# The last attention and the int8 feed forward of a decoder, from two loops one after the other to one loop with a turn per sequence

## The chip, the cores and the metric

The kernel runs on one core of a Trainium2 chip. A core has five engines with a queue each: TensorE (PE) multiplies matrices and writes to the banks of PSUM; VectorE (DVE), ScalarE (ACT) and GpSimd (POOL) work element by element, the first two also on PSUM; SyncE (SP) issues transfers (DMA). An engine works through its queue in order, and where an instruction needs another engine's result it waits on a semaphore, with all that is behind it. The metric is the time of one execution on the device, in microseconds (us); the time before is the median of three runs.

## The reference, cut to what matters

The model is a decoder of four layers, each an attention, a second attention over a context and a feed forward, twelve stages in all. Behind every stage comes `x = layernorm(x + stage(x))`. There are 16 sequences of 128 tokens with 256 features, in float32. The change touches the last two stages:

```python
def L3_xattn(q, k, v, gamma):             # q = x, k = v = context; (16, 128, 256)
    # eight heads over the middle axis: 16 tokens to a head; the softmax runs over the 256 features
    qh = q.reshape(B, 8, 16, 256); kh = k.reshape(B, 8, 16, 256); vh = v.reshape(B, 8, 16, 256)
    sm = softmax(einsum('bhdq,bhdl->bhql', qh, kh) / sqrt(16), axis=-1)
    return gamma * einsum('bhql,bhdl->bhdq', sm, vh).reshape(B, 128, 256)

def L3_ffn(x, W1, B1, W2, B2):            # 256 -> 1024 -> 256
    X1_q, sX1 = quantize_rowwise(x)       # round(x * 127 / absmax of the token)
    W1_q, sW1 = quantize_global(W1)       # one absmax for the whole matrix
    X2 = gelu((X1_q @ W1_q.T) * (sX1 * sW1 / 127**2) + B1)
    X2_q, sX2 = quantize_rowwise(X2)
    W2_q, sW2 = quantize_global(W2)
    return (X2_q @ W2_q.T) * (sX2 * sW2 / 127**2) + B2

x = layernorm(x + L3_xattn(x, ctx, ctx, gamma))
x = layernorm(x + L3_ffn(x, W1, B1, W2, B2))
```

Every sequence goes through these two stages by itself: nothing passes between sequences, except that the two weights are quantised once.

## The kernel before, in words

The whole activation `X` (128 tokens on the partitions, 16 sequences, 256 features) stays in on-chip memory. `run` opens the stages in order, each with pools of its own; the weights of a stage are loaded while the stage before it works. PSUM's eight banks are shared out by stage: in stage 10 the pool behind `ps` has six (bankA in the profile), the one behind `pt` two (bankB). A bank is given out in turn and can be written again when the reader of its last content is done.

**Stage 10, the attention** (`width_attention`, `width_unit`). One unit is one sequence `b`, written as a generator whose `yield`s cut it into pieces:

- the loads of three 256 KB context tiles by SP (L1857 to L1859);
- two pieces of score maxima: PE multiplies X with `eo` into four banks, DVE reduces each bank to a maximum in `npad`;
- PE transposes `npad`, DVE adds the maxima to the masked X (`xp`);
- two pieces of scores: eight matmuls into four banks, and four exponentials by ACT into `e`;
- two pieces of values: 16 matmuls of `vp` and `e` into one bankB, which ACT copies to `o`;
- PE transposes `o`, DVE takes reciprocals `rr` of the sums, POOL spreads them times gamma into `rw`;
- PE transposes `rw`, DVE multiplies (`y`), POOL adds both halves of `y` to X.

`rota` writes the order out by hand: in turn `n` it takes one piece of unit `n - lag` for each lag in a list. `Ordered` keeps each engine to that order; SP's transfers are left free. Behind every fourth unit `finish_in_turns` normalises four sequences: moments on DVE, the power -1/2 on POOL, the normalisation on DVE, and eight transposes with two ACT copies into `xT`. Buffers are three to five deep, `npad` and `rw` three each.

**Stage 11, the feed forward** (`s11`). First the weights: for each of the two matrices DVE finds the largest magnitude of each partition, POOL the largest over partitions, DVE scales and rounds (adding and subtracting `MAGIC`, L2306 and L2308). Then groups of four sequences: DVE quantises the tokens (`quantise`, L1953 to L1960: maximum, reciprocal, scaling, `t`, rounding `q`), PE transposes, ACT copies (`xqT`); then for each sequence PE multiplies with W1 into two banks, DVE scales and adds the bias (`h`, L2328), ACT applies gelu (L2332), DVE quantises the 1024 hidden values, PE transposes them in eight blocks, ACT copies (`hqT`, L2340), PE multiplies with W2, DVE scales and adds the bias (`y`, L2345), POOL adds to X (L2346). Behind each group come the normalisation and one 512 KB output transfer (L451). Nothing here is held to the written order.

A line of the profile can be a helper's: all ordered instructions have L321, so they are told apart by their tiles.

Of the kernel before, what the change touches and what calls it, by code (L numbers as in the profile page):

```python
# [12 lines left out]
F32 = mybir.dt.float32  # L13
BF16 = mybir.dt.bfloat16
# [6 lines left out]
NB = 16  # L21
S = 128
D = 256
# [300 lines left out]
class Decoder:  # L324
# [141 lines left out]
    def run(self):  # L466
# [4 lines left out]
        weights = {}  # L471
# [1362 lines left out]
    def s10(self, wk, w, last):  # L1834
        self.width_attention(wk, self.row("s10_gamma"), last)

    def width_attention(self, wk, gamma, last):
        nc = self.nc
        npad = [wk.tile([128, 512], F32, name=f"npad7_{n}", bufs=1) for n in range(3)]
        rw = [wk.tile([128, 2, 2, 128], F32, name=f"rw7_{n}", bufs=1) for n in range(3)]  # L1840
        for t in npad + rw:
            nc.gpsimd.memset(t, 0.0)
        self.nc = Ordered(self.tc, nc)
        rota(
            [self.width_unit(wk, gamma, npad[b % 3], rw[b % 3], b, last) for b in range(NB)],
            [0, 1, 3, 2, 4, 1, 3, 2, 4, 1, 5, 6, 7],
        )
        self.nc = nc

    def width_unit(self, wk, gamma, npad, rw, b, last):  # L1850
        nc = self.nc
        scale = 0.25
        eo = wk.tile([128, 2, D], F32, tag="eo7", name="eo7", bufs=3)
        e1 = wk.tile([128, 2, D], F32, tag="e17", name="e17", bufs=4)
        vp = wk.tile([128, 2, 8, 32], F32, tag="vp7", name="vp7", bufs=5)
# [4 lines left out]
        yield  # L1860
        xb = self.X[:, b, :]
# [17 lines left out]
        xp = wk.tile([128, 2, D], F32, tag="xp7", name="xp7", bufs=3)  # L1879
# [6 lines left out]
        e = wk.tile([128, 2, 4, 2, D], F32, tag="e7", name="e7", bufs=3)  # L1886
# [19 lines left out]
        o = wk.tile([128, 2, D], F32, tag="o7", name="o7", bufs=3)  # L1906
# [22 lines left out]
        if b % 4 == 3:  # L1929
            yield  # L1930
            yield from self.finish_in_turns(b // 4, last)
# [362 lines left out]
    def s11(self, wk, w, last):  # L2294
        nc = self.nc
        wq, sw = {}, {}
        for n in ("w1", "w2"):
            src = w[n].rearrange("p a b -> p (a b)")
            am = wk.tile([128, 1], F32, name=f"am_{n}", bufs=1)
            nc.vector.tensor_reduce(am, src, AX.X, ALU.max, apply_absolute_value=True)  # L2300
            al = wk.tile([128, 1], F32, name=f"al_{n}", bufs=1)
            nc.gpsimd.partition_all_reduce(al, am, 128, bass_isa.ReduceOp.max)
            s = wk.tile([128, 1], F32, name=f"s_{n}", bufs=1)
            nc.vector.reciprocal(s, al)
            nc.vector.tensor_scalar(s, s, 127.0, None, ALU.mult)
            nc.vector.tensor_scalar(src, src, s, MAGIC, ALU.mult, ALU.add)  # L2306
            q = wk.tile(list(w[n].shape), BF16, name=f"q_{n}", bufs=1)
            nc.vector.tensor_scalar(q, w[n], MAGIC, None, ALU.subtract)  # L2308
            nc.vector.tensor_scalar(al, al, 1.0 / (127.0 * 127.0), None, ALU.mult)
            wq[n], sw[n] = q, al  # L2310
        for g in range(NG):
            xq, am, _ = self.quantise(wk, self.X[:, 4 * g : 4 * g + 4, :], "11x")
            c1 = self.sm(4, tag="c111")
            nc.vector.tensor_scalar(c1, am, sw["w1"], None, ALU.mult)
            p = self.pt(2, 4, 128, dtype=BF16)
            for j in range(4):
                for k in range(2):
                    nc.tensor.transpose(p[:, k, j, :], xq[:, j, 128 * k : 128 * k + 128], self.identb)
            xqT = wk.tile([128, 2, 4, 128], BF16, tag="xqT11", name="xqT11")
            nc.scalar.copy(xqT, p)  # L2320
            for j in range(4):
                b = 4 * g + j
                h = wk.tile([128, 1, 1024], F32, tag="h11", name="h11")
                for n in range(2):
                    p = self.ps(512)
                    for k in range(2):
                        self.mm(p, xqT[:, k, j, :], wq["w1"][:, k, 512 * n : 512 * n + 512], k, 2)
                    nc.vector.scalar_tensor_tensor(  # L2328
                        h[:, 0, 512 * n : 512 * n + 512], p, c1[:, j : j + 1],
                        self.row("s11_b1")[:, 512 * n : 512 * n + 512], ALU.mult, ALU.add,  # L2330
                    )
                nc.scalar.activation(h, h, AF.Gelu_apprx_tanh)  # L2332
                hq, am2, _ = self.quantise(wk, h, "11h")
                c2 = self.sm(1, tag="c211")
                nc.vector.tensor_scalar(c2, am2, sw["w2"], None, ALU.mult)
                p = self.pt(8, 128, dtype=BF16)
                for k in range(8):
                    nc.tensor.transpose(p[:, k, :], hq[:, 0, 128 * k : 128 * k + 128], self.identb)
                hqT = wk.tile([128, 8, 128], BF16, tag="hqT11", name="hqT11")
                nc.scalar.copy(hqT, p)  # L2340
                p = self.pt(D)
                for k in range(8):
                    self.mm(p, hqT[:, k, :], wq["w2"][:, k, :], k, 8)
                y = wk.tile([128, D], F32, tag="y11", name="y11")
                nc.vector.scalar_tensor_tensor(y, p, c2, self.row("s11_b2"), ALU.mult, ALU.add)  # L2345
# [20 lines left out]
```

## Time and profile before

| what | value |
|---|---|
| median of 3 runs | 4087.18 us (4083.28 to 4091.48) |
| the profiled execution | 4093.2 us |
| its span in the profile | 4091.4 us |
| first matmul of stage 10 | at 3781.9 us |
| last addition to X in stage 10 | ends at 3951.0 us |
| first h of stage 11 | at 3965.7 us |
| last normalisation of stage 11 | ends at 4087.3 us |
| table loads on ACT from 3640 us to the end | 1 |

The profile is of one execution. Times of instructions count from the start of its span. The busy time of an engine is the time in which it works; its waits are put down to the instruction of another engine that came last. The two stages of the change are the last 310 us; everything ahead of them, 92% of the span, is the same code in both kernels. The clock granted to PE stands beside the windows, as a share of full speed.

### The profile page before, as it was taken

How to read it: one execution, taken by the hardware profiler on the slowest of the kernel's cores; microseconds unless marked ns; L12 is line 12 of the kernel's file. 1: busy time of each engine (PE TensorE's matmuls, PEld its weight loads, DVE VectorE, ACT ScalarE, POOL GpSimd, SP SyncE). 2: the span in 40 equal slices, each digit the busy share in tenths (PEclk: the TensorE clock that was granted, in tenths of full speed). 3: DMA queues.
4: the chain of work that ended last, by engine and by line, in shares of the span. 5: the costliest groups of instructions: out<-in, count | busy, mean ns of one | idle time of the engine just before them, and what ended most of it. 6: DMA issues, size and time to landing. Idle time of an engine off the chain costs nothing.

```text
span 4091.4 us, 96512 instructions
## 1 busy us (share of the span) xinstructions
PE 3615.8 (88%) x39274; PEld 2188.1 (53%) x39282; DVE 2572.0 (63%) x5650; ACT 2022.5 (49%) x4535; POOL 1846.0 (45%) x2036
## 2 busy tenths in 40 slices
PE   6999999999998716798989989888999999998975
PEld 4666666566565404565446655564454554554543
DVE  3767677677774464565235547665677666675776
ACT  2666666666665212343124544425565665564442
POOL 1444444444443135752135542204786666666221
PEclk8999999999999857899979999988999999999986
DMA  2111111111110001100010012101111111111200
GB/s 81 35 36 41 35 36 39 35 38 37 35 40 20 29 1 42 43 12 15 0 60 27 27 65 94 61 1 50 35 40 40 40 40 35 40 40 59 88 17 21
DMA packets 120649, 156.47 MB, mean 38 GB/s; under 512 B 15440, under 2 KB 79696, under 8 KB 119824
## 3 DMA queue, kind: packets, MB, share of 16 engines
q1 hardware_dynamic: 114352, 143.59, 11.4%
q8 instruction: 311, 5.10, 0.5%
q10 hardware_dynamic: 5712, 5.19, 0.4%
q0 software_dynamic: 144, 1.52, 0.1%
q14 instruction: 130, 1.06, 0.1%
HBM read 131.64 MB, written 2.10 MB: 33 GB/s over the span
## 4 chain that ended last, share of the span: by engine, by line
PE 76%; DVE 10%; ACT 5%; POOL 5%; issue 2%; DMA 1%; SPq 0%; ACTq 0%; POOLq 0%; DVEq 0%
PE bankA L321 39%; PE bankB L321 20%; PE bankC L321 8%; PE bankA L462 5%; PE bankB L462 4%; ACT accq L321 1%; DVE X L321 1%; ACT ot L321 1%; ACT gT L321 1%; POOL var L321 1%; DVE npad L321 1%; POOL t L321 1%; PE bankB L427 0%; POOL ln_rs L402 0%; ACT eb L321 0%
## 5 line engine op out<-in xcount | busy, mean ns | idle before, releaser
L321 PE MATMUL bankA<-xT,wzx 128*128 128x512 f32 x1024 | 458.5, 601 | 0.0
L321 DVE SCALAR_TENSOR_TENSOR acc<-bankA,half,acc 128x508 f32<-128x508 f32 (+2 forms) x384 | 285.2, 743 | 168.1 <-ACT acc L321 159.1
L321 POOL TENSOR_TENSOR m<-m,gm 128x512 f32<-128x512 f32 x256 | 318.1, 1278 | 45.3 <-ACT m L321 45.3
L321 PEld LDWEIGHTS bankA<-xT,wzx 128*128 128x128 f32 x1024 | 190.2, 191 | 227.2 <-issue 188.9
L321 PE MATMUL bankA<-xT,wkq 128*128 128x512 f32 x512 | 259.7, 632 | 0.0
L321 POOL TENSOR_TENSOR gT<-yx,sz 128x512 f32<-128x512 f32 x128 | 160.6, 1275 | 211.9 <-DVE yx L321 211.8
L321 PE MATMUL bankA<-xT,wvg 128*128 128x512 f32 x512 | 250.5, 612 | 0.2 <-issue 0.2
L321 POOL TENSOR_TENSOR eb<-eb,c_tri_s 128x512 f32<-128x512 f32 x64 | 81.3, 1271 | 375.3 <-ACT eb L321 375.3
L321 ACT ACTIVATE e<-bankA 128x512 f32<-128x512 f32 x320 | 165.2, 602 | 158.8 <-PE bankA L321 158.7
L321 DVE TENSOR_REDUCE npad<-bankA 128x2 f32<-128x512 f32 (+1 forms) x320 | 198.5, 684 | 60.9 <-PE bankA L321 60.6
L321 PE MATMUL bankC<-gT,wo 128*128 128x512 f32 x512 | 233.4, 599 | 2.7 <-POOL gT L321 2.7
L321 ACT ACTIVATE m<-bankA 128x512 f32<-128x512 f32 x256 | 132.1, 603 | 157.4 <-PE bankA L321 157.4
L321 POOL TENSOR_TENSOR sq<-sq,s 128x512 f32<-128x512 f32 x124 | 157.8, 1272 | 58.5 <-ACT s L321 53.8
L321 POOL TENSOR_SCALAR rs_ve<-o_mv 128x4 f32<-128x4 f32 x64 | 34.6, 540 | 291.7 <-DVE o_mv L321 291.7
L321 DVE SCALAR_TENSOR_TENSOR vT<-th,accv 128x512 f32<-128x512 f32 x64 | 45.6, 712 | 185.6 <-ACT th L321 185.6
L321 PEld LDWEIGHTS bankB<-y,tt 32*32 32x32 f32 x8192 | 87.0, 107 | 123.6 <-issue 88.5
L321 DVE SCALAR_TENSOR_TENSOR yx<-xs,cols,bankB 128x512 f32<-128x512 f32 x128 | 95.1, 747 | 91.9 <-PE bankB L321 86.3
L321 DVE SCALAR_TENSOR_TENSOR acck<-bankA,half_cols,acck 128x508 f32<-128x508 f32 (+2 forms) x192 | 142.5, 742 | 13.3 <-ACT acck L321 6.9
L321 PEld LDWEIGHTS bankC<-gT,wo 128*128 128x128 f32 x512 | 93.8, 192 | 99.3 <-issue 94.4
L321 DVE SCALAR_TENSOR_TENSOR accq<-bankA,half_cols,accq 128x508 f32<-128x508 f32 (+2 forms) x192 | 142.3, 741 | 4.5
L321 DVE SCALAR_TENSOR_TENSOR accv<-bankA,half_cols,accv 128x508 f32<-128x508 f32 (+2 forms) x192 | 140.0, 729 | 4.5
L321 ACT ACTIVATE acc<-bankA,half 128x512 f32<-128x512 f32 x128 | 100.7, 787 | 83.0 <-PE bankA L321 83.0
(482 smaller groups left out, 9321.9 us busy)
## 6 DMA issues: line engine op xcount, KB each, us to landing
wzx<-in_s_wzx SPq DMA_DIRECT2D x64, 512.0 KB
up<-cums SPq DMA_DIRECT2D x1152, 2.0 KB
wkq<-in_s_w SPq DMA_DIRECT2D x64, 256.0 KB
wvg<-in_s_w SPq DMA_DIRECT2D x64, 256.0 KB
wo<-in_s_wo SPq DMA_DIRECT2D x64, 128.0 KB
sw<-qraw SPq DMA_DIRECT2D x64, 128.0 KB
eo<-in_ctx_eo SPq DMA_DIRECT2D x32, 256.0 KB
e<-in_ctx_e SPq DMA_DIRECT2D x32, 256.0 KB
```

The source lines that it names most:

```text
L321: return lambda *a, **k: self.tc.keep_in_program_order(f(*a, **k))
L462: self.nc.tensor.matmul(out, lhsT=lhsT, rhs=rhs, start=(k == 0), stop=(k == n - 1))
```

## The change

Stage 10 (when it isn't the last) now runs both stages. A unit is a pair for one sequence: `width_unit` for the attention, `s11_unit` for the feed forward, and `weave` runs their pieces in an order of 21 places, `(which, lag)`, written out by hand. In turn `n` the place `(A, 1)` takes the next piece of the attention of sequence `n - 1`, and `(B, 9)` one of the feed forward of sequence `n - 9`. `s11` itself then does nothing.

```diff
     def s10(self, wk, w, last):
-        self.width_attention(wk, self.row("s10_gamma"), last)
...
+        npad, rw = self.width_zeros(wk, 1, 1)
+        _, w11 = self.weights[11]
+        with self.tc.tile_pool(name="kk11", bufs=2, side="right") as wk11:
+            self.nc = Ordered(self.tc, nc)
+            first = self.s11_weights(wk11, w11)
+            units = [
+                (
+                    self.width_unit(
+                        wk, self.row("s10_gamma"), npad[b % len(npad)], rw[b % len(rw)], b, None,
+                        [2, 3, 4, 2, 2, 1], first,
+                    ),
+                    self.s11_unit(wk11, w11, b),
+                )
+                for b in range(NB)
+            ]
+            A, B = 0, 1
+            weave(units, [
+                (A, 1), (A, 4), (A, 0), (B, 9), (A, 1), (B, 6), (A, 3), (B, 9), (A, 3), (B, 7), (B, 5),
+                (A, 2), (A, 1), (B, 4), (A, 3), (B, 6), (B, 7), (B, 5), (A, 1), (B, 5), (B, 4),
+            ])
```

Read by pieces, a turn holds in this order: A's first maxima (lag 1), the product and additions (4), the loads (0), B's last moments (9), A's second maxima (1), gelu (6), the first values (3), the last normalisation and output (9), the second values and the copy `o` (3), the transposes of the hidden values and `hqT` (7), the quantisation of the tokens (5), the second scores (2), the transposes of `npad` and `xp` (1), the first moments (4), the transposes of `o`, `rr` and `rw` (3), the quantisation of the hidden values (6), the second product, `y` and the addition (7), the transposes of the tokens and `xqT` (5), the first scores (1), the matmuls and `h` (5), the first normalisation (4).

The attention's unit keeps its work, with three differences. Its buffers are fewer (`npad` and `rw` one each, `eo` 2, `e1` 3, `vp` 4, `xp` 2, `e` 2, `o` 1). In the first maxima's piece it takes one step of the weights' preparation, as long as there is one. And it doesn't normalise: the `finish_in_turns` behind every fourth unit, with its transposes into `xT`, is gone.

```diff
         yield
+        if more:
+            next(more, None)
...
-        if b % 4 == 3:
+        if b % 4 == 3 and last is not None:
             yield
             yield from self.finish_in_turns(b // 4, last)
```

The feed forward goes by single sequences, and some of DVE's work goes to POOL: both roundings of the quantisation, the rounding of the weights, the two scalings `c1` and `c2`, and the normalisation.

```diff
+    def layernorm(self, b):
+        xb = self.X[:, b, :]
+        mv, rstd = self.moments([xb], 1e-5, "ln")
+        yield
+        self.nc.gpsimd.tensor_scalar(xb, xb, mv[:, 0, 0:1], rstd[:, 0:1], ALU.subtract, ALU.mult)
+
+    def quantise_row(self, wk, src, m, tag, bufs):
...
+        nc.vector.tensor_reduce(am, src, AX.X, ALU.max, apply_absolute_value=True)
+        nc.vector.reciprocal(s, am)
+        nc.vector.tensor_scalar(s, s, 127.0, None, ALU.mult)
+        t = wk.tile([128, m], F32, tag="t" + tag, name="t" + tag)
+        nc.vector.tensor_scalar(t, src, s, MAGIC, ALU.mult, ALU.add)
+        q = wk.tile([128, m], BF16, tag="q" + tag, name="q" + tag, bufs=bufs)
+        nc.gpsimd.tensor_scalar(q, t, MAGIC, None, ALU.subtract)
+        return q, am
+
+    def s11_unit(self, wk, w, b, norm=True):
...
+            yield from self.layernorm(b)
+            yield
+        xq, am = self.quantise_row(wk, xb, D, "11x", 1)
+        c1 = self.sm(1, tag="c111")
+        nc.gpsimd.tensor_scalar(c1, am, w["s1"], None, ALU.mult)
+        yield
...
+        xqT = wk.tile([128, 2, 128], BF16, tag="xqT11", name="xqT11", bufs=1)
+        nc.scalar.copy(xqT, p)
+        yield
...
+            nc.vector.scalar_tensor_tensor(h[:, cs], p, c1, self.row("s11_b1")[:, cs], ALU.mult, ALU.add)
+        yield
+        nc.scalar.activation(h, h, AF.Gelu_apprx_tanh)
+        yield
+        hq, am2 = self.quantise_row(wk, h, 1024, "11h", 1)
...
+        yield
...
+        hqT = wk.tile([128, 8, 128], BF16, tag="hqT11", name="hqT11", bufs=1)
+        nc.scalar.copy(hqT, p)
+        yield
...
+        nc.vector.scalar_tensor_tensor(y, p, c2, self.row("s11_b2"), ALU.mult, ALU.add)
+        nc.gpsimd.tensor_tensor(xb, xb, y, ALU.add)
+        yield
+        yield from self.layernorm(b)
+        nc.sync.dma_start(self.out[b], xb)
```

The weights' preparation (`s11_weights`) is a generator too, of four steps: for each matrix, first the maxima (DVE, POOL), then the scaling (DVE) and the rounding (now POOL). The output goes out in 16 transfers of 128 KB. The arithmetic of both stages is the same.

## The prediction

> **What bounds the kernel now.** I read the page first. Its shares (PE 88%, DVE 63%) are averages over twelve stages, and only the last two change, so next I cut the end of the span into windows. Columns: start:end, length, then busy us of PE, weight loads, DVE, ACT and POOL with counts, the granted clock, DMA share, GB/s.
>
> ```profile
> 3823.00:3850.00 27.00, 27.00 (x296) 14.80 (x288) 20.68 (x41) 14.15 (x27) 7.94 (x12) 1.00 0.30 90
> 3951.00:3967.00 16.00, 5.63 (x22) 3.31 (x24) 15.39 (x35) 3.47 (x4) 2.50 (x4) 0.50 0.00 1
> 3967.00:4087.00 120.00, 63.03 (x336) 38.22 (x336) 91.16 (x218) 35.78 (x35) 19.00 (x24) 0.63 0.04 14
> ```
>
> The first window is the attention in full flow: PE busy all of it at full clock, a sequence every 8.77 us in the timeline. The second prepares the feed forward's weights: DVE alone. The third is the feed forward: DVE busy 76%, PE only 53% at clock 0.63, 7.5 us a sequence. So the attention is bound by PE and the feed forward by DVE and its waits, one after the other. The attention's first matmul starts at 3781.9 and the span ends at 4091.4: the part that changes takes 309.5 us. Everything before 3781.9 is the same code.
>
> Next, the groups by shape in the last stages, and POOL's groups in the whole kernel (busy us, mean ns of one | idle before), for the price of each instruction:
>
> ```profile
> L321 DVE TENSOR_REDUCE npad<-bankA 128x2 f32<-128x512 f32 x128 | 79.4, 684 | 21.0 <-PE bankA L321 21.0
> L321 ACT ACTIVATE e<-bankA 128x512 f32<-128x512 f32 x128 | 66.1, 602 | 62.3 <-PE bankA L321 62.3
> L2328 DVE SCALAR_TENSOR_TENSOR h<-bankA,c,rows 128x512 f32<-128x512 f32 x32 | 22.4, 744 | 0.0
> L1953 DVE TENSOR_REDUCE am11h<-h 128x1 f32<-128x1024 f32 x16 | 19.1, 1212 | 0.1
> L1959 DVE TENSOR_SCALAR t11h<-h,s11h 128x1024 f32<-128x1024 f32 x16 | 11.9, 744 | 0.0
> L321 POOL TENSOR_SCALAR gT<-gT 128x512 f32<-128x512 f32 x64 | 96.1, 1501 | 23.7 <-ACT gT L321 18.9
> L321 POOL TENSOR_SCALAR xd<-xd,qsx 128x256 f32<-128x256 f32 x16 | 18.4, 1150 | 46.8 <-DVE xd L321 20.0 <-PE bankB L321 18.0 <-DVE xp L321 8.5
> L1569 POOL TENSOR_SCALAR d<-d5i 128x1280 f32<-128x1280 int32 x1 | 3.5, 3452 | 3.3 <-PE bankB L321 3.3
> L2346 POOL TENSOR_TENSOR X<-X,y 128x256 f32<-128x256 f32 x16 | 13.7, 856 | 103.1 <-DVE y L2345 86.8 <-DVE s11h L1954 13.1 <-DVE s11x L1954 3.1
> ```
>
> **The change, engine by engine.** A full turn holds one attention unit and one feed forward unit, in a fixed order on every engine. I summed what a turn costs each engine, back to back (a group of four reductions takes 2.42 us before the next may start, since neighbours overlap by some 0.07).
>
> DVE: 8 reductions 4.84; attention's y 0.61, xp 0.81, two reciprocals 0.24; two sets of moments 0.55 each, 1.10; the token quantisation 1.15 (a 256-wide reduction about 0.40 as an estimate between the 0.16 of the smallest operations and the 1.21 of 1024, reciprocal and scaling 0.16 each, t 0.34, gaps); the hidden quantisation 2.30 (1.21, 0.16, 0.16, 0.74); y 0.42; two h 1.34. Sum **12.8 us**. Left out are the last roundings (0.71 and 0.28) and the normalisation (0.41), which go to POOL.
>
> PE, at full clock: attention 8.0 (2.5 score maxima, 2.2 scores, 2.0 values, 1.3 transposes, from the timeline of one 8.77 us period), feed forward 2.8 (0.9 for the four h matmuls, of which nine stand in 2.11; 1.05 for the second product, 0.85 for ten transposes): 10.8. The 32 transposes into xT and 8 ACT copies that followed the attention go too; nobody reads them. At clock 0.79 (the window 3790 to 3810 had it) it would be 13.7.
>
> ACT: 8 exponentials 4.12, o 0.55, gelu 1.06, hqT 1.01, xqT 0.38 (the 128x256 copies take 0.37 to 0.38), sum 7.1. Exponential and gelu need different tables, shown by the load before the first gelu, so a turn adds two loads. The timeline prices one:
>
> ```profile
> 2766.43 1.06 ACT L2058 ACTIVATE parts<-parts 128x1024 f32<-128x1024 f32 x1 [3.54 <-DVE parts L2057]
> 2767.50 1.28 ACT L2059 ACT_TABLE_LOAD   x1
> 2768.80 1.06 ACT L2059 ACTIVATE parts<-parts 128x1024 f32<-128x1024 f32 x1
> ```
>
> The load starts when the activation before it ends and the next one starts as it ends, so a switch is 1.28 and ACT is 9.7 a turn (7.1 if one table held both). I take 9.7: below DVE, so hidden.
>
> The Trainium skill speaks against this: "ScalarE: Activation LUTs", section "What ACT_TABLE_LOAD costs", puts a drain of about 1.38 us on top of the 1.28 and advises batching by table set. By that, ACT would be 12.5 a turn, close under DVE. The rows above show no such gap.
>
> POOL: two X additions 1.54; two rsqrt pairs 0.83 each (the small scaling 0.23; the power by its rows of 2, 4 and 16 columns, 0.75, 1.04, 2.90, so 0.6 for one); two normalisations at the 1.15 of the 128x256 row with two operations; two rw 1.19; the last addition 0.73; two one-column scalings 0.48. The roundings have no row. The 512 and 1280 rows lie on 2.54 ns an element plus 0.2, so 1024 costs 2.8 and 256 costs 0.85; by the 256 row times four it would be 4.6 and 1.15. I take the first, as 1024 lies between its two rows, and keep the other. Sum **11.6**, or 13.7.
>
> The skill's "GPSIMD Engine Reference", section "4.1 Engine selection", calls one-input elementwise work roughly line-rate on POOL. The 1.50 us for 512 elements above says otherwise; at line rate POOL would be about 9.5 a turn and never in question.
>
> **What is not on any engine's list: DVE waiting for POOL.** A scaling of one column takes 0.15 us alone (of four, 0.17 at 3869.0), and 0.71 beside a POOL addition, ending with it:
>
> ```profile
> 3972.28 0.15 DVE L1955 TENSOR_SCALAR s11h<-s11h 128x1 f32<-128x1 f32 x1
> ...
> 3992.33 0.72 POOL L2346 TENSOR_TENSOR X<-X,y 128x256 f32<-128x256 f32 x1 [3.14 <-DVE s11x L1954]
> 3992.37 0.71 DVE L1955 TENSOR_SCALAR s11x<-s11x 128x4 f32<-128x4 f32 x1
> ```
>
> A turn has four such DVE operations (two scalings, t of 256, t of 1024) beside a POOL that is busy some 85% of it. Found behind a POOL instruction at random, each waits about 0.38 (squares of POOL's durations without the long rounding, which comes after t, over twice their sum): 4 x 0.38 x 0.85 = 1.3. It could be 0, or 4 x 1.15 = 4.6. So a full turn is 12.8 + 1.3 = **14.1 us**.
>
> **Do the waits between engines fit in that?** From the first reduction (t = 0): DVE has the second four done by 6.0, token quantisation by 7.2 to 8.2, xp by 9.0; PE does xq's transposes and the scores by 10.5, ACT the exponentials behind them, and the next maxima need those banks: 11.3 to 12.2 for the round, inside 14.1. The added waits: POOL's rounding q11x holds PE at xq's transposes, and behind them in PE's queue the scores and h matmuls, then ACT's exponentials; POOL's rounding q11h (ready about 1 us into the next turn) is needed at 3. Single npad, rw, o, hqT and xqT buffers are rewritten only after their reader's place in the order. SP gets 16 output DMAs among its loads; a load has a whole turn to land (256 KB pieces, 81 GB/s in flow now), so I cost it at nothing, and if the cover went, a turn would wait for its load's landing, seen as DMA before bankA.
>
> **The sum.** Turn 1 starts at 3781.9 as now.
> Filling, turns 1 to 5: attention alone makes a round of about 8.7 (reductions 4.9, transposes 0.65, xp 0.87, scores to the first bank 0.9, exponential 0.7, next maxima 0.6); with the weights' preparation (2.28 and 1.28 twice; the first beside idle DVE at 3780 to 3784; POOL rounds 2048 in 5.4, late in turn 4): 8.7 + 9.0 + 9.3 + 11.5 + 10.5 = 49.
> Turns 6 to 8, by DVE's 11.8, 12.2, 12.3 and 1.2 each: 39.9.
> Turns 9 to 16: 8 x 14.1 = 112.8.
> Draining: no maxima any more, so POOL sets turns 17 to 19 (11.5, 11.5, 10.3), then chains: 8.0, 6.5, 4.4; the last moments and normalisation 2.6; last output 4.1, as the span now ends 4.1 after the last normalisation. Together 58.9.
> Sum 260.6 against 309.5: 48.9 less. The profiled execution of 4093.2 (span 4091.4) becomes 4044. It lies 6 above the median of the runs, 4087.18, so the median becomes **4038**.
>
> **Rivals.**
> *No port waits* (the 0 above): turns shorter by 1.2 to 1.3, 11 of them: 14 less, **4024**. For it: most xs operations beside a busy POOL in the stage before take 0.68; against: some take 1.28.
> *POOL is the bound:* by the 256 row a turn of POOL is 13.7, with 0.7 of waits behind DVE's t and 0.8 for DVE's results 15.2: 11 x 1.1 = 12, and 8 more in draining, **4058**. For it: nothing has been rounded to bf16 on POOL here. Against: the 512 and 1280 rows.
> *PE's queue goes head-blocked, and it is slower:* bankB has two banks and a turn takes seven from it; PE stops at each until the reader two back is done. In the feed forward now PE waits on ACT's hqT each time:
>
> ```profile
> PE bankB L462 <- ACT hqT L2340: 18.4, 16, 1.2
> DVE y L2345 <- PE bankB L462: 18.0, 13, 2.4
> ```
>
> If all seven cost up to 1.3 and nothing hid them, a turn is 10.8 + 9.1 = 19.9, 11 x 5.8 = 64 more, **4102**. It decides from 18.5 a turn, where 11 x 4.4 eats the 48.9. Half of it gives 17, 4070. Against it: PE has 3 us to spare a turn and the order puts other work between.
> *The change doesn't overlap as it says* (table loads are in the way): if one table holds both, ACT drops to 7.1 and the time stays; if the two halves still followed each other, a sequence would cost 8.77 + 7.5 and 2.6 of loads, 18.9; 16 of them 302, with some 8 to fill 310, which is **4088**, no change.
>
> **Numbers.** Chances: forecast 0.50, no port waits 0.20, POOL 0.18, head-blocked 0.08 (half of it past the deciding point), no overlap 0.04. The range 4013 to 4068 takes in the first three with their bounds (clean turns and 1 us less in each fill and drain turn below; POOL and 1 us a turn of waits above) and leaves out the rest and some of the ends. A measurement here can tell about 0.2%, 8 us: faster by more 0.93, within 0.02, slower 0.05.
>
> **What would show it.** In the changed profile: a turn of 13 to 15 between reductions, DVE busy over 85% in the full turns, POOL over 75%; two table loads a turn, 1.28 each, with no DVE wait behind them; q11h near 2.8 (at 4.6, POOL binds); DVE's t and scalings longer than 0.74 and 0.15 beside POOL; PE's clock above 0.79. Wrong if DVE is idle over 3 us a turn, and the release it waits for names the culprit: bankA by PE, X by POOL, bankB.

## The result, and the profile after

The changed kernel takes **4036.14 us** (median of 4 runs, 4030.13 to 4039.38) against 4087.19 for the kernel before: ratio **0.987** [0.986, 0.989], 51 us faster. The forecast was 4038. Executed again beside later experiments it took 4041.68 against 4088.61, ratio 0.988 [0.987, 0.990].

The profiled execution took 4038.81 us, its span 4037.0. The attention's first matmul starts at 3780.1, so the changed part, called the *tail* from here on, went from 309.5 us to **256.9**. The start of the tail wanders by some microseconds from one execution to the next (3771 to 3785 in the runs below, in code that none of them changes), so I compare tails. Its length comes from the first matmul and the span; a turn's length is the spacing of the first reduction into `npad` of one sequence and the next, in the timeline.

First the same cut as before: windows of the changed kernel in full turns, in turns 17 to 19, and at the end (start:end, length, busy us of PE, weight loads, DVE, ACT, POOL with counts, clock, DMA share, GB/s).

```profile
3894.00:3957.00 63.00, 58.21 (x572) 33.83 (x570) 61.62 (x141) 47.88 (x70) 59.51 (x76) 1.00 0.19 62
3970.00:4000.00 30.00, 17.47 (x145) 9.88 (x138) 17.38 (x44) 13.64 (x17) 28.53 (x36) 0.74 0.03 10
4000.00:4037.00 37.00, 13.51 (x65) 6.63 (x63) 16.32 (x37) 5.78 (x7) 29.86 (x36) 0.55 0.06 21
```

The first line is five turns of 12.64. DVE is busy 98% of it and POOL 94%, PE 92% at full clock: nearly everything is in use at once, where before PE was full in the attention, and DVE 76% and PE 53% busy in the feed forward. The second and third lines are the draining: DVE falls to 58% and 44%, POOL stays at 95% and 81%.

Then the groups by shape, over the tail (busy us, mean ns of one | idle before):

```profile
L321 DVE TENSOR_REDUCE npad<-bankA 128x2 f32<-128x512 f32 x128 | 78.7, 678 | 5.6 <-PE bankA L321 5.5
L321 POOL TENSOR_SCALAR q11h<-t11h 128x1024 bf16<-128x1024 f32 x16 | 44.4, 2776 | 2.0 <-DVE t11h L321 0.8
L321 POOL TENSOR_SCALAR X<-X,ln_mv,ln_rs 128x256 f32<-128x256 f32 x32 | 39.3, 1230 | 1.8
L321 ACT ACT_TABLE_LOAD x25 | 32.1, 1283 | 0.5
L321 POOL TENSOR_SCALAR rw<-rr,rows 128x128 f32<-128x128 f32 x32 | 24.2, 767 | 7.0 <-DVE npad L321 7.0
L321 DVE TENSOR_SCALAR t11h<-h,s11h 128x1024 f32<-128x1024 f32 x16 | 13.3, 833 | 0.6
L321 POOL TENSOR_SCALAR q<-w 128x2048 bf16<-128x2048 f32 x2 | 10.8, 5385 | 7.7 <-issue 7.7
```

The reductions waited 21.0 us for PE before and wait 5.6 now. The rounding q11h takes 2.776, as estimated. DVE's t11h is only 0.09 over the 0.744 of before: there is little waiting at the shared path of DVE and POOL. ACT's table loads are there, and the timeline of ACT, one turn, shows what they cost:

```profile
3917.13 2.06 ACT L321 ACTIVATE e<-bankA 128x512 f32<-128x512 f32 x4 [0.57 <-PE bankA L321]
3919.22 1.28 ACT L321 ACT_TABLE_LOAD   x1
3920.51 1.06 ACT L321 ACTIVATE h<-h 128x1024 f32<-128x1024 f32 x1
3923.96 0.58 ACT L321 COPY o<-bankB 128x512 f32<-128x512 f32 x1 [2.39 <-PE bankB L321]
3924.54 1.01 ACT L321 COPY hqT<-bankB 128x1024 bf16<-128x1024 bf16 x1
3925.57 1.28 ACT L321 ACT_TABLE_LOAD   x1
```

Each load starts as the instruction before it ends and takes 1.28; then ACT has 2.39 us to wait for PE anyway. Last, POOL through the same turn:

```profile
3918.47 2.77 POOL L321 TENSOR_SCALAR q11h<-t11h 128x1024 bf16<-128x1024 f32 x1
...
3925.00 0.23 POOL L321 TENSOR_SCALAR rs_ve<-ln_mv 128x1 f32<-128x1 f32 x1
3925.31 0.57 POOL L321 TENSOR_TENSOR ln_rs<-rs_ve,c_neghalf 128x1 f32<-128x1 f32 x1
3925.99 1.23 POOL L321 TENSOR_SCALAR X<-X,ln_mv,ln_rs 128x256 f32<-128x256 f32 x1
3927.31 0.85 POOL L321 TENSOR_SCALAR q11x<-t11x 128x256 bf16<-128x256 f32 x1
...
3929.39 1.64 POOL L321 TENSOR_SCALAR rw<-rr,rows 128x128 f32<-128x128 f32 x2
3931.11 2.77 POOL L321 TENSOR_SCALAR q11h<-t11h 128x1024 bf16<-128x1024 f32 x1
```

No line names a wait, yet 3925.00 + 0.23 is not 3925.31. Eight of POOL's 15 starts in a turn come 0.08 to 0.11 us after the end of the instruction ahead. Four of the eight (the second addition, both powers, a normalisation) read what the one ahead has just made; the other four (both rs_ve, q11x, q11h) read what DVE had finished at least 0.5 us before, so why they come late stays open. They add up to 0.7 a turn: POOL works 11.94 and its turn is 12.64. DVE has eight late starts too, of 0.035 us each, all of them behind a result of its own:

```profile
3925.44 0.41 DVE L321 TENSOR_REDUCE am11x<-X 128x1 f32<-128x256 f32 x1
3925.88 0.16 DVE L321 RECIPROCAL s11x<-am11x 128x1 f32<-128x1 f32 x1
3926.08 0.15 DVE L321 TENSOR_SCALAR s11x<-s11x 128x1 f32<-128x1 f32 x1
3926.27 0.41 DVE L321 TENSOR_SCALAR t11x<-X,s11x 128x256 f32<-128x256 f32 x1
```

Its turn is 12.36 of work and 0.28 in these starts, with no other gap. Both engines look full. In the draining it is POOL alone; the chain of the end, from 3970 to 4008, holds nothing else:

```profile
by line: POOL X L321 35.9%; POOL q11h L321 29.2%; POOL q11x L321 9.7%; issue 7.6%; POOL ln_rs L321 6.4%; POOL rw L321 6.4%; POOL c L321 4.4%; POOL rs_ve L321 3.6%; POOLq L321 0.3%
```

### The profile page after: what moved, and what is told of

It reads as the page before. It is cut to its first block, busy times and chain, and to the rows that moved or that the text cites. A ratio compares the mean times of both kernels' runs of the same rounds, so it can differ in the third digit from the quotient of the medians.

```text
span 4037.0 us, 96594 instructions
## 1 busy us (share of the span) xinstructions
PE 3591.9 (89%) x39250; PEld 2174.9 (54%) x39250; DVE 2549.9 (63%) x5600; ACT 2047.0 (51%) x4563; POOL 1977.4 (49%) x2178
## 4 chain that ended last, share of the span: by engine, by line
PE 74%; DVE 11%; POOL 6%; ACT 5%; issue 2%; DMA 1%; SPq 0%; ACTq 0%; POOLq 0%; DVEq 0%
PE bankA L321 38%; PE bankB L321 19%; PE bankC L321 8%; PE bankA L462 5%; PE bankB L462 3%; DVE npad L321 2%; ACT accq L321 1%; ACT ot L321 1%; ACT gT L321 1%; POOL var L321 1%; DVE X L321 1%; POOL t L321 1%; POOL X L321 1%; PE bankB L427 0%; DVE ln_st L321 0%
## 5 line engine op out<-in xcount | busy, mean ns | idle before, releaser
L321 DVE SCALAR_TENSOR_TENSOR acck<-bankA,half_cols,acck 128x508 f32<-128x508 f32 (+2 forms) x192 | 142.5, 742 | 14.1 <-ACT acck L321 7.7
```

The lines of the kernel that those rows point to most:

```text
L321: return lambda *a, **k: self.tc.keep_in_program_order(f(*a, **k))
```

## The experiments

The theory after the first look at the result: the gain is the overlap alone; in full turns DVE sets the pace at 12.64, with hardly any waits for POOL; in the draining POOL sets it; table loads are hidden. Rivals: POOL sets the full turns too; or ACT does, by its table loads. All kernels below are the changed one with the edit shown. Times of one column come from different chips, so the ratio to the kernel before, run on the same chip, is what to compare; "last" is the time from turn 16's first reduction to the end.

| kernel | time, us | ratio | tail | full turn | turns 1 to 5 | last |
|---|---|---|---|---|---|---|
| changed | 4036.14 | 0.987 [0.986, 0.989] | 256.9 | 12.64 | 51.1 | 79.6 |
| the same again | 4041.68 | 0.988 [0.987, 0.990] | 258.7 | 12.64 | 52.9 | 79.6 |
| one more reduction on DVE | 4047.20 | 0.988 [0.986, 0.991] | 263.0 | 13.1 | 52.0 | 79.9 |
| two more powers on POOL | 4051.98 | 0.990 [0.988, 0.992] | 269.1 | 13.8 | 51.7 | 84.3 |
| tanh for gelu | 4039.31 | 0.987 [0.984, 0.989] | 257.7 | 12.67 | 51.6 | 79.7 |
| POOL's share back on DVE | 4041.83 | 0.988 [0.985, 0.990] | 263.5 | 14.2 | 51.3 | 70.9 |
| not woven | 4123.00 | 1.008 [1.006, 1.009] | 339.7 | 9.2, then 10.1 | | |
| draining on DVE | 4021.35 | 0.983 [0.981, 0.985] | 242.4 | 12.64 | 51.1 | 65.1 |
| c1, c2 on ACT | 4038.87 | 0.987 [0.986, 0.989] | 257.0 | 12.67 | 52.9 | 77.3 |
| several at once | 4024.15 | 0.984 [0.983, 0.986] | 246.7 | 13.14 | 48.7 | 63.7 |
| both ends on DVE | 4019.75 | 0.983 [0.982, 0.985] | 239.7 | 12.65 | 48.5 | 64.9 |

**Is it the overlap?** The same pieces, each half in an order of its own, one loop after the other.

```diff
-            weave(units, [
-                (A, 1), (A, 4), (A, 0), (B, 9), ...
-            ])
+            rota([u[0] for u in units], [1, 4, 0, 1, 3, 3, 2, 1, 3, 1])
+            rota([u[1] for u in units], [5, 2, 5, 3, 1, 0, 2, 3, 1, 1, 0])
```

> The same pieces, buffers and engines, but all attention units first and then all feed forward units, each in its own part of the order. If the gain is the overlap, it goes with it: the attention alone some 9 us a sequence and 12 to fill, 156, then the feed forward by POOL's 9.5 us a sequence and 20 to fill and drain, 172: tail 328, 18 above the kernel before (309.5), time near 4108. If the gain came from moving DVE's work to POOL and dropping the transposes, the tail stays under 295.

The tail is 339.7, 30.2 longer than before the change. The window of its feed forward says why:

```profile
3935.00:4080.00 145.00, 70.44 (x326) 32.90 (x331) 84.96 (x207) 35.14 (x44) 124.99 (x150) 0.53 0.03 10
```

POOL is busy 86% of it and a sequence takes 10.1, where the feed forward before took 7.5 and kept POOL busy 16% of the time. So the change has two halves: sequence by sequence with DVE's work moved to POOL **costs 30**, and weaving **gives 83** back. Only the sum is a gain. (The kernel without weaving differs from the one before also in its fewer buffers and in the written order of its feed forward; no run separates these, so the 30 belongs to all of them together.)

**Which engine sets the full turn?** One reduction of a score bank more on DVE, with a result that nobody uses; then two powers of one column more on POOL, likewise unused.

```diff
+            if more is not None and mc == 1:
+                junk = self.sm(2, tag="junk7")
+                nc.vector.tensor_reduce(junk, banks[3], AX.X, ALU.max, negate=True)
```

> One more reduction of a bank by DVE (0.61 us) in each attention unit's second maxima; its result is not used. The tail, from the attention's first matmul to the end of the span, is 256.9 us in the changed kernel. If DVE sets the full turns, each of the 11 turns from 6 to 16 grows by 0.61 (12.64 to 13.25) and the tail by 6.7, to 263.6; turns 1 to 5 have idle DVE that hides it. If POOL (94% busy in full turns) sets them, DVE's addition goes into slack: 0 to 1.

```diff
+        if more is not None:
+            junk = self.sm(2, tag="junk7")
+            for k in range(2):
+                nc.gpsimd.tensor_tensor(junk[:, k : k + 1], self.ones, self.neghalf[:, :1], ALU.pow)
```

> Two more one-column powers by POOL (0.57 us each) in each attention unit's last piece; their results are not used. If DVE sets the full turns and POOL has the 0.7 us a turn that it shows idle, the first 0.7 are free and 0.4 are paid in some 9 full turns, and all 1.14 in the three POOL-bound turns of the drain: 7 more, tail 264. If POOL already sets the full turns: 1.14 in 9 full turns and 3 of the drain, 14 more, tail 271. If POOL sets neither: 0.

Both make the turn longer. DVE's 0.68 (some 0.6 back to back) gives 0.46: the shift takes t11x and t11h out of POOL's way, and they get 0.14 shorter (0.353 and 0.786 for 0.415 and 0.865). POOL's 1.15 gives all of 1.15. Windows of one length in full turns, for the first of these kernels, then for the second:

```profile
3900.00:3950.00 50.00, 45.17 (x444) 26.11 (x448) 48.99 (x111) 36.47 (x54) 46.04 (x59) 1.00 0.23 75
```

```profile
3900.00:3950.00 50.00, 42.32 (x428) 24.05 (x424) 45.80 (x107) 34.48 (x51) 47.46 (x64) 1.00 0.18 59
```

With more on DVE, POOL falls to 92% and DVE stays at 98%; with more on POOL, DVE falls to 92% and POOL rises to 95%, which with its late starts is all it can. In the first, POOL's q11x comes 0.48 us after the instruction ahead and DVE has its 0.28 of late starts and no other gap; in the second, DVE idles 1.0 to 1.1 us a turn ahead of an h and POOL has its 0.7 and nothing more. My "DVE sets the pace" was half the story: **both engines are full at 12.64** and whichever gets more sets the turn.

**Is the moved work worth it?** Both roundings and both normalisations back from POOL to DVE.

```diff
-        self.nc.gpsimd.tensor_scalar(xb, xb, mv[:, 0, 0:1], rstd[:, 0:1], ALU.subtract, ALU.mult)
+        self.nc.vector.tensor_scalar(xb, xb, mv[:, 0, 0:1], rstd[:, 0:1], ALU.subtract, ALU.mult)
...
-        nc.gpsimd.tensor_scalar(q, t, MAGIC, None, ALU.subtract)
+        nc.vector.tensor_scalar(q, t, MAGIC, None, ALU.subtract)
```

> The two roundings of the tokens and hidden values and both normalisations go back from POOL to DVE; the weave stays. If DVE sets the full turns, each costs 0.71 + 0.28 + 0.82 - 0.2 = 1.6 more (14.2) in 11 turns, 18 more, and the drain, which POOL sets, gets 15 shorter: tail 260. If POOL sets the full turns, they get shorter or stay with the drain shorter by 15: tail 242 or less.

DVE gets 0.81 + 0.69 + 0.29 a turn, and the turn goes to 14.2; POOL is left with 6.4. Turns 6 to 15 get 15.1 longer. But the part after turn 16's start is 8.6 *shorter* (70.9), since draining has no maxima and DVE has time there. The tail is 263.5, so the moved work is worth 6.6; in time that is within the intervals (0.988 and 0.987).

**Are the table loads hidden?** Tanh in gelu's place, so that one table serves both.

```diff
-        nc.scalar.activation(h, h, AF.Gelu_apprx_tanh)
+        nc.scalar.activation(h, h, AF.Tanh)
```

> Tanh in gelu's place, so that ACT needs one table for both stages; the feed forward's activation is another function and its output not the reference's. ACT does 2.57 us less a turn. If DVE sets the full turns they stay at 12.6 and the tail changes by 0 to -4 (loads in filling and draining): 253 to 257. If the table loads are on the path, as the rule of batching by table has it, up to 2.57 x 11 = 28 less, tail 229.

The turn is 12.67, the tail 257.7. In 50 us of full turns ACT is busy 27.9 us where the changed kernel has 37.9, and nothing gets faster. Hidden, to 0.03 a turn.

**Draining on DVE.** The last sequences' roundings and normalisations (the last two to five, by the operation), by the finding that DVE has time there.

```diff
+        by = self.nc.vector if dve else self.nc.gpsimd
+        by.tensor_scalar(xb, xb, mv[:, 0, 0:1], rstd[:, 0:1], ALU.subtract, ALU.mult)
...
-            yield from self.layernorm(b)
+            yield from self.layernorm(b, b >= 13)
...
-        xq, am = self.quantise_row(wk, xb, D, "11x", 1)
+        xq, am = self.quantise_row(wk, xb, D, "11x", 1, nc.vector if b >= 12 else None)
...
-        hq, am2 = self.quantise_row(wk, h, 1024, "11h", 1)
+        hq, am2 = self.quantise_row(wk, h, 1024, "11h", 1, nc.vector if b >= 11 else None)
...
-        yield from self.layernorm(b)
+        yield from self.layernorm(b, b >= 14)
```

> For the last sequences only, where DVE has nothing of the attention left to do, roundings and normalisations go back to DVE: hidden values from sequence 11, tokens from 12, the first normalisation from 13, the last one from 14. If POOL sets the drain (12.5 us a turn in turns 17 to 19, POOL 95% busy), these turns fall to 8.5 to 9.5 and the last ones by 2 each: drain 66.9 to about 52, tail 242, time about 4021. If the drain is a chain of waits between engines, the tail falls by less than 5.

Tail 242.4: 14.5 less, 14.4 of it behind turn 16's start. This kernel is faster than the changed one too: its interval [0.981, 0.985] lies below that of the changed kernel, [0.986, 0.989]. From 3970 to 4000 DVE is now busy 92% and POOL 79%.

**Can the balance be pushed further?** First the two one-column scalings from POOL to ACT, beside the unchanged kernel as a mark.

```diff
-        nc.gpsimd.tensor_scalar(c1, am, w["s1"], None, ALU.mult)
...
         nc.scalar.copy(xqT, p)
+        c1 = self.sm(1, tag="c111")
+        nc.scalar.activation(c1, am, AF.Copy, scale=w["s1"])
...
         nc.scalar.copy(hqT, p)
+        c2 = self.sm(1, tag="c211")
+        nc.scalar.activation(c2, am2, AF.Copy, scale=w["s2"])
```

> The changed kernel once more, unchanged, as the mark for the two beside it. Every theory expects a tail (first matmul of the attention to the end of the span) of 256.9 us, a full turn of 12.64 and a ratio to the kernel before of 0.987.

> The two one-column scalings c1 and c2 go from POOL to ACT, behind the copies xqT and hqT. Theory 'two engines bind': in the changed kernel's turn of 12.64 POOL is busy 11.94 and each of its some 12 starts comes about 0.06 after the end before it, so POOL has no slack at all, while DVE is busy 12.36. Two scalings of 0.30 with their gaps take 0.7 off POOL, DVE is left, and a full turn becomes about 12.4; turns 17 to 19 go from 12.5 to 11.8. Tail 256.9 - 8 x 0.24 - 3 x 0.7 = 253. Theory 'DVE alone binds': the full turn stays 12.64, only the drain gains 2, tail 255. Theory 'ACT's place matters': two more ACT instructions ahead of the exponentials make the turn longer than 12.64, tail over 257.

POOL's work falls from 11.94 to 11.43 a turn, and the turn is 12.67, with DVE at 12.39 of work and the same 0.28 of late starts. POOL now waits for DVE, once each in every one of four turns; in the changed kernel's list of the same window neither line stands (waits from 3900 to 3950: us in total, times, longest):

```profile
POOL rs_ve L321 <- DVE rr L321: 1.6, 4, 0.4
POOL q11x L321 <- DVE t11x L321: 1.2, 4, 0.3
```

So DVE's 12.64 is as full as POOL's, and there was no 0.2 to gain: the expectation of 12.4 had taken DVE's 0.28 for slack. ACT's added 0.6 can hide no gain either, since DVE idles for nobody. The drain gained 2.2, about what the first two theories said. The tail is no shorter than 257.0 because turns 1 to 5 took 52.9, as in the unchanged kernel beside it.

That difference of 1.8 in the filling needs no change of code. The window of the changed kernel's first execution, then that of its second, at the same place of the tail:

```profile
3792.00:3802.00 10.00, 9.42 (x62) 6.99 (x59) 8.79 (x13) 5.08 (x10) 5.40 (x1) 0.78 0.18 54
```

```profile
3793.00:3803.00 10.00, 9.42 (x52) 7.49 (x51) 7.52 (x11) 3.02 (x6) 5.40 (x1) 0.50 0.19 54
```

PE is busy for the same 9.42 us, but at a granted clock of 0.78 in one and 0.50 in the other: 62 matmuls against 52. Turns 2 and 3 are 8.6 each in the first, 11.2 and 11.1 in the second; turn 4 gives 3.3 of these 5.1 back (9.2 for 12.5): POOL's rounding of the second weight starts 0.7 us after that turn has begun, and not 3.2. Of the eleven profiled executions with this filling, two had 0.50 at this place (this one and that of c1, c2 on ACT), and only these two have a turn 2 of 11.2; the nine others had 0.78 or 0.79 and turns of 8.5 to 8.6.

Then several edits at once: the draining on DVE, c1 and c2 on ACT, both weights' roundings on DVE, and the token scaling on ACT.

```diff
+        if m == D and b < 12:
+            nc.scalar.activation(t, src, AF.Copy, scale=s, bias=MAGIC)
+        else:
             nc.vector.tensor_scalar(t, src, s, MAGIC, ALU.mult, ALU.add)
```

> The kernel with the last sequences' roundings and normalisations on DVE (tail 242.4), with c1 and c2 on ACT, the token scaling t11x (0.42 on DVE) on ACT up to sequence 11, and both weights' roundings on DVE. If DVE and POOL bind together, a full turn becomes 12.36 - 0.42 and some gaps, about 12.05, on DVE and 11.9 on POOL: nine turns by 0.55 less, 5 us. Turn 4, now 12.5 behind POOL's 5.4 us rounding of the second weight, falls to about 9.5: 3 us. Tail 242.4 - 8 = 234, time about 4013. If the rounding in turn 4 was hidden and ACT's two added waits (for DVE's maxima) hold back its exponentials, the turn stays at 12.6 and the tail near 240, time 4019.

Missed: tail 246.7, not 234. The filling gained 2.4, and DVE and POOL both got lighter (12.17 and 11.47 a turn), but the turn is 13.14. ACT in this kernel:

```profile
3933.17 1.01 ACT L321 COPY hqT<-bankB 128x1024 bf16<-128x1024 bf16 x1
3934.08 0.30 ACT L321 ACTIVATE c<-am11h,al 128x1 f32<-128x1 f32 x1
3934.68 0.51 ACT L321 ACTIVATE t11x<-X,s11x 128x256 f32<-128x256 f32 x1 [0.30 <-DVE s11x L321]
3935.21 1.28 ACT L321 ACT_TABLE_LOAD   x1
3936.51 2.06 ACT L321 ACTIVATE e<-bankA 128x512 f32<-128x512 f32 x4
```

In the changed kernel the load follows hqT at once, while DVE is still at the token's maximum. Here t11x stands ahead of it and waits for DVE, so the load begins only then, and the exponentials, xqT, the h matmuls and DVE's h come behind. Over 15 us of full turns the chain of waits of this kernel holds the load with 8.6% and ACT's e with 16.6%. ACT is busy 10.3 of 13.14, so it is no engine that binds here but a *place* in a queue: a **hidden load is shown again by a waiting instruction ahead of it**. c1 and c2 alone on ACT left the turn at 12.67, so it is t11x that makes the difference. How much of the 0.5 is the load, and how much t11x itself and its wait, no run separates.

So the last kernel keeps only what touches the two ends, and leaves ACT alone: draining and its c1, c2 on DVE, and both weights' roundings on DVE.

```diff
-            nc.gpsimd.tensor_scalar(q, src, MAGIC, None, ALU.subtract)
+            nc.vector.tensor_scalar(q, src, MAGIC, None, ALU.subtract)
...
-        nc.gpsimd.tensor_scalar(c1, am, w["s1"], None, ALU.mult)
+        (nc.vector if b >= 12 else nc.gpsimd).tensor_scalar(c1, am, w["s1"], None, ALU.mult)
...
-        nc.gpsimd.tensor_scalar(c2, am2, w["s2"], None, ALU.mult)
+        (nc.vector if b >= 11 else nc.gpsimd).tensor_scalar(c2, am2, w["s2"], None, ALU.mult)
```

> Only the two ends of the changed kernel: the last sequences' roundings and normalisations on DVE (the kernel of tail 242.4), with their scalings c1 and c2 on DVE too, and both weights' roundings on DVE. Nothing is added to ACT. Theory 'POOL holds the ends': turns 2 to 4, 29.7 together (31.5 where the clock of PE comes back late), lose the wait of the attention's rw behind POOL's 5.4 us rounding, about 2.5; the drain loses the gaps of POOL's scalings, about 1.5; full turns stay 12.64. Tail about 238.5, time about 4018. Theory 'PE holds the filling': the 5.4 us were beside transposes and scores that wait for PE at half clock, turns 2 to 5 stay the same and the tail is 241.

Turns 1 to 5 fall to 48.5, 2.6 less: turn 4 goes from 12.5 to 8.7 and turn 3, where DVE now rounds, from 8.6 to 9.9. So POOL's rounding of the second weight was on the path of turn 4. The scalings in the draining gave 0.2, not 1.5: with the rest on DVE, POOL was busy only 79% there. Tail 239.7, 17.2 under the changed kernel; in time it can't be told from the draining kernel (0.983 both).

**Why did DVE not wait for POOL?** Two small programs without the decoder: DVE does a run of one kind of instruction, while POOL does a run of another kind, or nothing. "ts" is the scaling t over 1024 columns, "red" the reduction of 1024.

```diff
+                    for _ in range(12):
+                        nc.vector.tensor_scalar(dt, src, one[:, 0:1], MAGIC, ALU.mult, ALU.add)
...
+                        nc.gpsimd.tensor_scalar(po, pin, MAGIC, None, ALU.subtract)
```

> No decoder: runs of one DVE instruction (t of 1024, a one-column scaling, a reduction, an operation with two inputs in SBUF) beside runs of one POOL instruction (none, addition of 256, normalisation of 256 with two scalars, one-column power, rounding of 1024 to bf16, spreading like rw); the output is the input. As the prediction priced it, any POOL instruction holds DVE's t and scaling to its end: t grows from 0.74 by 0.4 or more beside each of the five. By the changed kernel's trace (scalings 0.15 beside POOL's normalisation, t 0.86 beside rw) only the addition, which has two inputs, holds them fully; beside the others t grows by under 0.2 and the scaling not at all. The reduction (one input) grows beside none.

```profile
L321 DVE TENSOR_SCALAR d_ts_none<-src,one 128x1024 f32<-128x1024 f32 x12 | 9.0, 752 | 0.4
L321 DVE TENSOR_SCALAR d_ts_pow<-src,one 128x1024 f32<-128x1024 f32 x12 | 9.0, 753 | 0.4
L321 DVE TENSOR_SCALAR d_ts_norm<-src,one 128x1024 f32<-128x1024 f32 x12 | 10.0, 834 | 0.4
L321 DVE TENSOR_SCALAR d_ts_add<-src,one 128x1024 f32<-128x1024 f32 x12 | 13.0, 1084 | 0.4
L321 DVE TENSOR_SCALAR d_ts_round<-src,one 128x1024 f32<-128x1024 f32 x12 | 14.4, 1199 | 0.4
L321 DVE TENSOR_REDUCE d_red_round<-src 128x1 f32<-128x1024 f32 x8 | 9.7, 1219 | 0.2
L321 POOL TENSOR_SCALAR p_round_red<-pin 128x1024 bf16<-128x1024 f32 x5 | 13.9, 2771 | 0.3
L321 POOL TENSOR_SCALAR p_round_ts<-pin 128x1024 bf16<-128x1024 f32 x5 | 17.1, 3413 | 0.3
```

A scaling isn't held by powers, hardly by normalisations (834 for 752), but by additions and by roundings; a reduction by nothing. And it is mutual: the rounding grows from 2771 to 3413, and also the power, which leaves the scaling alone, takes 801 beside it and 550 beside the reduction. The second program asks how wide a DVE instruction must be to be held.

```diff
+        for dve, many in ((1, 60), (2, 60), (4, 60), (16, 60), (64, 40), (256, 24)):
...
+                    nc.vector.tensor_scalar(dt[:, :dve], src[:, :dve], one[:, 0:1], MAGIC, ALU.mult, ALU.add)
```

> No decoder: DVE runs the same scaling (t, one input) 60 times on 1, 2, 4, 16 columns, 40 times on 64 and 24 times on 256, each alone, beside POOL additions of 128x256 and beside POOL normalisations of 128x256. Theory 'width decides': one column takes 0.15 whatever POOL does, as the scalings of the changed kernel did, and from two or four columns on an instruction can be held for the rest of a POOL instruction, as the four-column scaling of 0.71 in the kernel before, so its mean beside additions is well over twice that alone. Rival 'length decides': up to 16 columns (0.17 alone) nothing is held, and 256 columns (0.35 alone) grow to 0.5 or more beside additions. Rival 'nothing is held': all widths the same beside POOL, and the four-column row was a single accident.

```profile
L321 DVE TENSOR_SCALAR d_c_add<-src,one 128x2 f32<-128x2 f32 x60 | 24.5, 408 | 2.1
L321 DVE TENSOR_SCALAR d_c_none<-src,one 128x2 f32<-128x2 f32 x60 | 13.7, 229 | 2.1
L321 DVE TENSOR_SCALAR d_c_add<-src,one 128x1 f32<-128x1 f32 x60 | 12.9, 215 | 2.1
L321 DVE TENSOR_SCALAR d_c_none<-src,one 128x1 f32<-128x1 f32 x60 | 12.9, 215 | 2.1
```

Width decides, and the step is between one column and two: 215 ns in any company, against 229 alone and 408 beside additions. The prediction's row was a four-column scaling, and the change's scalings have one.

## Why the prediction was right, and where it was not

The forecast of 4038 is 2 from the measured 4036, and its main step held: the halves overlap, and a full turn is about as long as DVE's list. But its full turn of 14.1 did not come; 12.64 is what the rival without port waits said, which had a chance of 0.20. That the time agrees so closely is luck: 15.9 us less in turns 6 to 16 stand against 12.2 more at the two ends. By its own steps (the predicted terms start at the first matmul, so the 2.1 us to the first reduction is counted to the filling):

| step | predicted | measured | what the runs showed |
|---|---|---|---|
| filling, turns 1 to 5 | 49 | 53.2 | 2.1 to the first reduction, then 51.1; turn 1 is 12.3 with the 2.1, not 8.7, at a PE clock of 0.50; 1.8 more in all where the clock rose late |
| turns 6 to 8 | 39.9 | 35.9 | hardly any port waits |
| turns 9 to 16 | 112.8 | 100.9 | 12.6 each, not 14.1 |
| draining | 58.9 | 66.9 | turns 17 to 19 36.5, not 33.3; behind them 30.4, not 25.6 |
| sum | 260.6 | 256.9 | |

*DVE's list, 12.8.* Work 12.36, of which some 0.2 is t11h and t11x being held (0.86 for 0.74, 0.42 for 0.35). The durations of its 28 instructions add to 13.96, and neighbours overlap by 1.6; I had allowed for only part of that, so the list was 0.6 too dear. The 0.28 of late starts was on no list.

*Port waits, 1.3: the step that was mis-sized.* 0.2 measured. Of the four DVE operations that I let wait, the two scalings have one column and aren't held by anything. The two others meet other partners than an addition in the full turns: t11x lies beside a normalisation and takes 0.42, but 0.77 in turns 17 to 19, where it lies beside additions. t11h lies beside POOL's spreading of rw, whose like left it at 752 ns in the small program and gave way itself (852 for 604), and in the kernel too rw gave way (0.62 and 1.04 in one turn). Why t11h takes 0.86 there all the same isn't shown. I priced one row, 0.71 of a four-column scaling, as if width and partner didn't matter.

*Rival "no port waits", 4024.* Right for the full turn, wrong in time, because it used my filling and my draining, together 12.2 too short.

*POOL's list, 11.6.* Work 11.94 and 0.7 of late starts: 12.64. Single prices held: q11h 2.77 for the estimated 2.8, q11x 0.86 for 0.85, the power 0.57 for 0.6. What I left out were the late starts; and two rw, priced at 1.19, take 1.64 in the full turns, where the second lies beside t11h. *Rival "POOL is the bound", 4058:* its price (4.6 for q11h) is refuted, its place is not: two more powers show that POOL has no slack, and the drain is POOL's.

*Draining, 58.9.* 66.9. "POOL sets turns 17 to 19" was right and 3.2 short (12.5, 12.5 and 11.5 by the starts of q11h), for the late starts and for q11x, which takes 1.19 there. The other 4.8 lie in the chains behind, most of them in the last one (14.3 for 11.1); why it is longer wasn't followed up. Moving POOL's work to DVE took off 14.4, the most that any of these edits gave.

*ACT, 9.7 with two loads.* 9.6, and the loads cost nothing (tanh: 12.67). 25 loads are shown, two in each turn that holds both halves. The rule of a 1.38 us drain, weighed in the prediction, found no row: 24 of the 25 loads are followed within 0.02 us by the next activation, and behind the last one gelu waits for DVE's h.

*PE, 10.8 at full clock.* 11.7 busy at a clock of 1.00. *Rival "head-blocked", 4102:* in 50 us of full turns the list of waits gives PE's bankB 3.8 us for DVE's xp and nothing else: 1 us a turn, in PE's spare time. *Rival "no overlap", 4088:* refuted by the turn; the kernel without weaving shows what it would have been, and it is worse than I priced (10.1 a sequence for the new feed forward, not 7.5).

*"SP's output transfers cost nothing":* no wait of the full turns names a transfer (the loads in flow are at 90 GB/s by the prediction's own first window, not at 81). *"POOL rounds 2048 in 5.4, late in turn 4":* 5.39, and worth 2.6.

## What to carry to other kernels

When two loops with different bottlenecks are woven into one, list each engine's work per turn with overlaps and start gaps, and expect the turn to be the fullest list; then look at the filling and the draining apart, for work that was moved to balance the full turn is in the wrong place there (here 14 us of 257, cured by a condition on the sequence number). A table load on an engine with time to spare was free here only as long as nothing ahead of it in that queue waited. And price a contention by rows with the same width and the same partner, or not at all.

## What the runs showed of the hardware that I had not expected

- *Being held needs two columns.* A DVE scaling of one column takes 215 ns alone, beside additions and beside normalisations; of two columns 229, 408 and 281. The Trainium skill, "VectorE: DVE Perf Modes", section "Mode 2×_2P", says of the mode that reads one tensor through both ports that it splits the outermost dimension that isn't one, which has to be even (or odd and equal in source and destination). A single column has no such dimension; the step measured here agrees with it.
- *It isn't held for the whole instruction.* The skill's "SBUF — State Buffer", section "Who interferes with whom", says that the one that starts first keeps the shared ports for its whole instruction and the other is fully blocked. Reductions left alone (1.219 in any company) agree. But beside POOL roundings of 2.77 no scaling took over 1.58 us, 0.83 more than alone, while the roundings grew by 0.5 to 0.8 when scalings ran beside them throughout: so they seem to take turns within one POOL instruction, which is inferred from these durations. In that run the measurement decides.
- *Engines start late with nothing to wait for.* Where a DVE instruction reads the result of the one ahead, it starts 0.035 us after its end; eight of POOL's 15 starts a turn come 0.08 to 0.11 us late, four of them behind a result of its own. The profile names no wait. It is 0.28 and 0.7 us in a turn of 12.64.
- *The clock in the filling is not fixed.* The same kernel had a granted clock of 0.78 in one execution and 0.50 in another at the same place, and turns 1 to 5 took 51.1 and 52.9 us.
